# A two-layer graph-attention kernel: x1's transposes and the scalings in another order, queries behind a row's first eaten tile, half of a mask on ScalarE

## The chip, the cores and the metric

The kernel runs on one core of a Trainium2 chip. The metric is the device time of one launch in microseconds. Five engines work side by side, each from a queue of its own that is kept in order, and synchronise by semaphores: TensorE (PE: matrix products and transposes, into PSUM), VectorE (DVE), ScalarE (ACT), GpSimd (POOL) and SyncE (SP), which here issues nearly all DMA transfers. SBUF holds tiles of 128 partitions[...].

## The reference

`x` is (8, 2048, 256) in fp32: eight batch entries of 2048 nodes with 256 features. `adj` is (2048, 2048) of 0 and 1, the same for all entries. Two layers, each with a residual and a layer norm:

```
# layer 0: 8 heads of 32
xp   = einsum('bnd,hdf->bhnf', x, W)
e    = leaky_relu(e_src[..., :, None] + e_dst[..., None, :], 0.2)   # e_src, e_dst = xp . a_src, a_dst
e    = e + softplus(beta) * log(adj + 1e-6);  e = where(adj > 0, e, -big)
h    = softmax(e) @ xp, heads side by side
x    = layernorm(x + h @ W_out.T)
# layer 1: one head of 256
e    = leaky_relu((x @ W1) @ (x @ W2).T, 0.2);  e = where(adj > 0, e, -1e12)
x    = layernorm(x + relu(softmax(e) @ (x @ W3)))
```

## The kernel before, in words

**Layer 0 ("Gat").** The exponential of the leaky sum of two terms is written as a product of factors per row and per column with one maximum, so that the attention of a head is made transposed, source nodes on partitions: a tile `s` for 128 source nodes and half of the target nodes (1024), two heads side by side. A `Unit` is one pair of heads and one half of the targets: 16 such tiles, 8 units per entry. For a tile, ACT scales the transposed mask `mt` by a factor of each head (`scale`, L478, two instructions), DVE takes the maximum with `c` and multiplies (`make`, L492, two), POOL adds the tile to a running sum for the denominator (L498, two), and PE multiplies it with the values (`eat`, L524 `val`). Five of the sixteen tiles (3, 6, 9, 12, 15) are "direct": DVE takes `mt` unscaled, POOL has nothing to do, and PE makes their part of the denominator (`den`). At the end of a unit `close` adds the sum's part (`den` of `ones`), and the values are copied out (L534, L545). The first `make` of a unit needs two copies of `c` into PSUM (L488).

**Layer 1 ("Dot").** A `step` is one row tile of 128 nodes, 16 per entry. `queries` makes h1 for four row tiles (L680, copies L682). `scores` makes a row's scores in four strips of 512 (L691, `e`), each put through leaky relu by ACT (`Prelu`, L693); DVE subtracts the mask and takes the row's maximum (L700), ACT takes the exponential with its sum (L702). `turned` transposes the result (L718, copies L720), and L742 multiplies it with h3 (`acc`). L743 to L750 apply relu, add x1 and take the statistics; `end_row` (L762 to L765) normalises.

**The mask.** Entry 1 of the program (index 0) makes `pen` from `adj` for each row (`mask`, L235 to L243) and stores it; the other entries load it.

**The order.** PE's order is as written in the program throughout. For the first layer of entry 1 a scheduler orders the other engines; from L849 on all engines keep the order of the program. From there a `Stream` feeds the tiles of the next entry's first layer between the instructions of an entry's second layer: `ahead` scales the tile after the next one and makes the next, `eat` multiplies one, `feed` does one of each. `between(c)` stands ahead of a strip's scores, `after(c)` behind its prelu. At the end of an entry stands a seam (L866 to L900): `rows` (L409 `y`, the residual L413, statistics L414) and `rows_scale` and `rows_end` (L420 to L431) make x1 by groups of four row tiles, `turn` transposes x1 (L448, copies L449) and makes h3 from it (L454, copies L456), and `Dot` starts the next second layer with its queries and its first scores, which have no row beside them. `turn` yields after each pair of row tiles; `lag` says by how many pairs h3 follows the transposes.

**Buffers.** `pt`, `e`, `acc`, h1, `y`, `tr` and h3 all take turns in two PSUM banks (tag `mm`, L89), so each of them waits until the tile before the last has been read out; only in the last entry's second layer, when the stream is over, are there six. `s` tiles share a ring of nine with `p` and one half of `ht`; `mt` has four buffers.

Of the kernel before, what the change touches and what calls it, by code (L numbers as in the profile page):

```python
# [9 lines left out]
F32 = mybir.dt.float32  # L10
BF16 = mybir.dt.bfloat16
I32 = mybir.dt.int32
AF = mybir.ActivationFunctionType
# [5 lines left out]
P = 128  # L19
# [1 line left out]
PRIOR_EPS = 1e-6  # L21
LN_EPS = 1e-5
FMAX = 3.4028234663852886e38
NO_EDGE = -3.0e38


@with_exitstack
def kernel(
# [69 lines left out]
    def ring_tile(name, shape=(P, N)):  # L98


        return wide.tile(list(shape), F32, tag="s", name=name, bufs=9)
# [14 lines left out]
    nc.vector.memset(ones, 1.0)  # L116
    eps_ln = const.tile([P, 1], F32)
    nc.vector.memset(eps_ln, LN_EPS)


    beta = const.tile([P, 4], F32)
# [107 lines left out]
    def mask(it, make):  # L229

        pen = wide_tile("pen", "pen", 1, BF16)
        if not make:
            nc.sync.dma_start(pen, pen_d[ts(it, P), :])
            return pen, lambda: None
        edges = [chunk.tile([P, HALF], I32, tag="ht", name="adj_r", bufs=4) for _ in range(2)]  # L235
        for s, a in enumerate(edges):
            nc.sync.dma_start(a, adj[ts(it, P), ts(s, HALF)])

        def put():
            for s, a in enumerate(edges):  # L240
                nc.vector.tensor_scalar(pen[:, ts(s, HALF)], a, 0.0, NO_EDGE, ALU.is_le, ALU.mult)
            nc.sync.dma_start(pen_d[ts(it, P), :], pen)
        return pen, put  # L243

# [16 lines left out]
    class Gat:  # L261


        def __init__(self, b):
            self.b = b
            self.ms, self.mts, self.v = [], [], {}

        def begin(self):

# [89 lines left out]
        def step(self, k):  # L359

            hp, k = divmod(k, NT)
            rh, j2 = divmod(k, J2)
            first = hp == 0
            if hp == NP - 1 and k == 0:
                gats[1].load_factors()
            if j2 == 0:
                self.unit = Unit(self, hp, rh)
            elif j2 == 2:
                stage_after(self.unit)
            if first:  # L370
                self.more_mt(k + 2, k > 0)
            mts = self.mts[k] if first else [load_mt(k, i) for i in range(2)]
            for i in range(2):
                self.unit.scale(2 * j2 + i, mts[i])
# [26 lines left out]
        def rows(self, g):  # L401


            self.load_rows(g + 2)
            self.st = st = small.tile([P, IG // 2, nc.vector.BN_STATS_DIM], F32, name="st4", bufs=2)
            ys = [mm_tile("y").rearrange("p (t c) -> p t c", t=2) for _ in range(IG // 2)]
            for k in range(IG):
                for kc in range(KC):
                    nc.tensor.matmul(ys[k // 2][:, k % 2, :], self.ht[kc][:, ts(g * IG + k, P)], wot[:, kc, :],  # L409
                                     start=(kc == 0), stop=(kc == KC - 1))  # L410
            for k, y in enumerate(ys):
                z = self.x1(2 * g + k)
                nc.vector.tensor_add(z, y, self.xs[g][:, ts(k, 2), :])  # L413
                nc.vector.bn_stats(st[:, k, :], z.rearrange("p t c -> p c t"))  # L414

        def rows_scale(self):

            mv = self.st.rearrange("p a (t c) -> p (a t) c", t=2)
            self.f = f = small.tile([P, 2, IG], F32, name="f4", bufs=2)
            nc.scalar.activation(f[:, 0, :], mv[:, :, 2], AF.Ln, bias=eps_ln, scale=1.0 / D)  # L420
            nc.scalar.activation(f[:, 0, :], f[:, 0, :], AF.Exp, scale=-0.5)
            nc.vector.scalar_tensor_tensor(f[:, 1, :], mv[:, :, 1], -1.0, f[:, 0, :], ALU.mult, ALU.mult)

        def rows_end(self, g):

            for k in range(IG):
                z, f = self.x1(2 * g + k // 2), self.f
                row = z[:, k % 2, :]
                nc.scalar.activation(row, row, AF.Identity, bias=f[:, 1, k:k + 1], scale=f[:, 0, k:k + 1])
                if k % 2:  # L430
                    nc.scalar.dma_start(x1_d[self.b].rearrange("(t p) d -> p t d", p=P)[:, ts(2 * g + k // 2, 2), :], z)  # L431
# [5 lines left out]
        def turn(self):  # L437
# [1 line left out]

            self.x1t = x1t = whole.tile([P, KC, N], F32, tag="x1t", name="x1t")  # L440
            self.h3 = h3 = whole.tile([P, NT, D], F32, tag="h3", name="h3")
            lag = 1 if self.b + 1 < B else 4
            for j in range(NT // 2 + lag):
                if j < NT // 2:
                    t = mm_tile("tr1")
# [15 lines left out]
    class Unit:  # L461
# [7 lines left out]
            self.s, self.mt = {}, {}  # L469
            self.val = self.den = self.sums = None  # L470

        def scale(self, jt, mt):

            self.mt[jt] = mt
            self.s[jt] = s = ring_tile("s", (P, HP, HALF))
            if jt not in self.direct:
                for a, h in enumerate(self.heads):
                    nc.scalar.activation(s[:, a], mt, AF.Copy, scale=self.gat.re[:, 1, jt, h:h + 1])  # L478

        def make(self, jt):  # L480

# [107 lines left out]
    class Stream:  # L589


        def __init__(self):
            self.units = [Unit(gats[b], hp, rh) for b in range(1, B) for hp in range(NP) for rh in range(2)]
            self.count = len(self.units) * NT
            self.loaded = self.scaled = self.made = self.eaten = 0
            self.held = False
            self.mts = {}

        def at(self, n):
# [66 lines left out]
    class Dot:  # L666
# [17 lines left out]
        def scores(self, it, between=lambda c: None, after=lambda c: None):  # L684
# [17 lines left out]
            nc.scalar.activation(p, p, AF.Exp, bias=neg, scale=-1.0, accum_out=den)  # L702
            self.ahead = den

        def step(self, stream, count, lead=0):
# [148 lines left out]
    for b in range(1, B + 1):  # L854
# [19 lines left out]
        for g in range(NB + 2):  # L874
# [61 lines left out]
```

## Time and profile before

| | |
|---|---|
| time, median of three runs | 4374.54 us (4362.75 to 4380.53) |
| the profiled execution's own time | 4372.4 us |
| its span, first to last instruction | 4370.6 us |
| granted TensorE clock, mean | 0.979 of full speed |
| first layer of entry 1 | 0 to about 513 us |
| then an entry's period (seam and 16 rows) | about 505 us |
| an ordinary row | 25.6 us |
| rows of the last entry, without a stream | from 4121 us, 15.5 us each |
| DMA | 843.63 MB, 193 GB/s in the mean |

The profile is of one execution. In the lists a line gives the source line, the engine, the operation and the tiles (out<-in), then how often, the busy time, the mean duration in ns and the idle time of the engine ahead of it with what ended it. In a timeline the columns are start, length, engine and instruction. A matmul in fp32 shows as two records. PE's busy time is modelled to the end of the pipeline, so that a gap of a few tenths between two groups doesn't show.

### The profile page before, as it was taken

Reading aid. Unit: us, or ns where it says so; the run is one execution under the profiler, and the core shown is the slowest. Engines: PE = TensorE matmul, PEld = TensorE weight load, DVE = VectorE, ACT = ScalarE, POOL = GpSimd, SP = SyncE. Lnnn points to the kernel's source line nnn. Section 1 sums busy time; section 2 is a strip of 40 time slices with the busy share of each in tenths; the row PEclk is TensorE's granted clock in tenths of the full one; section 3 lists DMA queues with packets and bytes.
Section 4 is the critical chain, followed back from the end, with each engine's and each line's share of the span. In section 5 each row is a group of like instructions: output and inputs, shape, how many; then the busy total and the mean of one; then the engine's idle time right before and its main releaser. Section 6 shows DMA issues by size and latency. Waiting matters only on the chain.

```text
span 4370.6 us, 60300 instructions
## 1 busy us (share of the span) xinstructions
PE 4126.0 (94%) x22704; PEld 2090.3 (48%) x22704; DVE 3334.9 (76%) x3278; ACT 2905.3 (66%) x4132; POOL 2888.3 (66%) x1190
## 2 busy tenths in 40 slices
PE   7899799998999999999899999999899999999999
PEld 4444344444444444445444454444444444444766
DVE  7888788988878887788777887788787787787222
ACT  6422466676677767677777776677677776776555
POOL 0000477877788887889788877888687887888000
PEclk9999999999999999999999999999999999999999
DMA  8888755666565565556556564656555565554211
GB/s 268 275 288 285 237 198 196 218 223 218 184 198 189 188 205 191 178 195 215 186 178 203 195 207 166 193 193 197 190 199 180 186 219 171 187 192 158 79 46 46
DMA packets 346437, 843.63 MB, mean 193 GB/s; under 512 B 49696, under 2 KB 166432, under 8 KB 346144
## 3 DMA queue, kind: packets, MB, share of 16 engines
q1 hardware_dynamic: 328736, 822.99, 57.4%
q10 hardware_dynamic: 17408, 16.78, 1.1%
q8 instruction: 178, 2.92, 0.3%
q14 instruction: 115, 0.94, 0.1%
HBM read 763.76 MB, written 75.37 MB: 192 GB/s over the span
## 4 chain that ended last, share of the span: by engine, by line
PE 66%; ACT 12%; DVE 9%; issue 6%; DMA 5%; POOL 1%; SPq 1%; ACTq 0%; DVEq 0%; POOLq 0%
PE e L691 18%; PE val L524 15%; PE acc L742 14%; PE den L524 6%; PE pt L718 5%; ACT s L478 5%; DVE s L492 5%; DMA mt<-mt_d 3%; PE h3p L454 3%; DVE p L700 2%; PE h1p L680 2%; ACT p L702 2%; PE y L409 2%; ACT c L488 1%; PE proj L294 1%
## 5 line engine op out<-in xcount | busy, mean ns | idle before, releaser
L498 POOL TENSOR_TENSOR sums<-sums,s 128x1024 f32<-128x1024 f32 x1008 | 2505.7, 2523 | 272.8 <-DVE s L492 271.9
L492 DVE SCALAR_TENSOR_TENSOR s<-c,re,s 128x1024 f32<-128x1024 f32 x1232 | 1500.8, 1272 | 269.9 <-ACT c L488 197.6
L478 ACT ACTIVATE s<-mt,re 128x1024 f32<-128x1024 f32 x1232 | 1339.8, 1140 | 49.9 <-DMA mt<-mt_d 38.7
L524 PE MATMUL val<-s,v 128*32 128x512 f32 x8192 | 1094.5, 607 | 30.7 <-DVE s L492 17.8
L691 PE MATMUL e<-x1t,h 128*128 128x512 f32 x2048 | 995.8, 610 | 45.9 <-ACT pts L720 30.4
L742 PE MATMUL acc<-h,pts 128*128 128x256 f32 x4096 | 918.3, 382 | 1.5 <-ACT pts L720 1.0
L742 PEld LDWEIGHTS acc<-h,pts 128*128 128x128 f32 x4096 | 770.4, 190 | 198.5 <-ACT p L693 29.3
L700 DVE CUSTOM_DVE_ANT_0 p<-p,pen 128x2048 f32<-128x2048 f32 x128 | 459.6, 3591 | 310.3 <-ACT p L693 310.1
L492 DVE SCALAR_TENSOR_TENSOR s<-c,re,mt 128x1024 f32<-128x1024 f32 x560 | 687.5, 1268 | 0.0
L498 POOL TENSOR_TENSOR sums<-s 128x1024 f32<-128x1024 f32 x112 | 291.9, 2629 | 412.4 <-DVE s L492 405.1
L693 ACT ACTIVATE p<-e 128x512 f32<-128x512 f32 x512 | 306.8, 599 | 383.4 <-PE e L691 383.4
L524 PEld LDWEIGHTS val<-s,v 128*32 128x32 f32 x8192 | 203.1, 109 | 683.2 <-issue 442.9
L691 PEld LDWEIGHTS e<-x1t,h 128*128 128x128 f32 x2048 | 356.0, 194 | 333.9 <-issue 258.9
L702 ACT ACTIVATE p<-p,neg 128x2048 f32<-128x2048 f32 x128 | 256.5, 2004 | 374.2 <-DVE neg L700 373.6
L524 PE MATMUL den<-s,re 128*32 128x512 f32 x3264 | 443.1, 594 | 0.0
L718 PEld LDWEIGHTS pt<-ident,p 128*128 128x128 f32 x2048 | 224.1, 142 | 456.0 <-ACT p L693 129.1
L718 PE MATMUL pt<-ident,p 128*128 128x128 f32 x2048 | 332.7, 287 | 73.1 <-ACT p L702 39.5
L492 DVE SCALAR_TENSOR_TENSOR s<-c_in,re,mt 128x1024 f32<-128x1024 f32 x256 | 310.2, 1277 | 51.6 <-DMA mt<-mt_d 39.5
L720 ACT COPY pts<-pt 128x512 f32<-128x512 f32 x512 | 294.5, 579 | 79.8 <-PE pt L718 79.0
L305 POOL PARTITION_ALL_REDUCE top<-top x8 | 6.6, 821 | 428.9 <-DVE top L304 412.5
L524 PEld LDWEIGHTS den<-s,re 128*32 128x32 f32 x3264 | 110.1, 110 | 244.6 <-issue 242.9
L745 DVE TENSOR_TENSOR z<-acc,x1r 128x256 f32<-128x256 f32 x128 | 54.0, 422 | 199.0 <-ACT acc L743 189.8
(96 smaller groups left out, 2493.7 us busy)
## 6 DMA issues: line engine op xcount, KB each, us to landing
mt<-mt_d SPq DMA_DIRECT2D x992, 512.0 KB
c_in<-c_d SPq DMA_DIRECT2D x64, 1024.0 KB
pen<-pen_d SPq DMA_DIRECT2D x112, 512.0 KB
xg<-in_x_dram SPq DMA_DIRECT2D x60, 512.0 KB
adj_t<-in_adj_dram SPq DMA_DIRECT2D x16, 1024.0 KB
mt_d<-mt SPq DMA_DIRECT2D x32, 512.0 KB
rb<-rec_d SPq DMA_DIRECT2D x128, 128.0 KB
x_d<-ht ACTq DMA_DIRECT2D x64, 256.0 KB
```

Source lines behind the costliest of these rows:

```text
L454: nc.tensor.matmul(t[:, ts(i, D)], x1t[:, kc, ts(2 * (j - lag) + i, P)], w3s[:, kc, :], start=(kc == 0), stop=(kc == KC - 1))
L478: nc.scalar.activation(s[:, a], mt, AF.Copy, scale=self.gat.re[:, 1, jt, h:h + 1])
L492: nc.vector.scalar_tensor_tensor(s[:, a], self.c[a], self.gat.re[:, 0, jt, h:h + 1], m, ALU.max, ALU.mult)
L498: nc.gpsimd.tensor_tensor(self.sums[:, a], of[:, a], s[:, a], ALU.add)
L524: nc.tensor.matmul(dst[ts(q, DH), :], weights[q % 2], s[:, q % 2, ts(q // 2, BK)], start=start, stop=stop)
L691: nc.tensor.matmul(t, self.h1[:, kc, ts(it % IG, P)], self.x1t[:, kc, ts(c, BK)], start=(kc == 0), stop=(kc == KC - 1))
L693: nc.scalar.activation(p[:, ts(c, BK)], t, AF.Prelu, alpha=ALPHA)
L700: nc.vector.tensor_tensor_reduce(p, p, pen, -1.0, FMAX, ALU.add, ALU.min, neg)
L702: nc.scalar.activation(p, p, AF.Exp, bias=neg, scale=-1.0, accum_out=den)
L718: nc.tensor.transpose(t[:, ts(k, P)], p[:, ts(g * IG + k, P)], ident)
L720: nc.scalar.copy(pt, t)
L742: nc.tensor.matmul(acc, pts[g][:, ts(k, P)], self.h3[:, j, :], start=(j == 0), stop=(j == NT - 1))
```

## The change

It has these parts, all of them from L849 on.

- **Scaling by head.** `Unit.scale` is split: `begin` takes the slot, `scale(jt, a)` scales one head. `Stream.scale_head` scales the first head of the next tile, `scale_next` what is left of it. In `step`, for strips 1 to 3 of the next row's scores, `scale_head` stands between the transposes' copy and that strip's prelu; the second head comes after the prelu as before. After the last strip, between the row's maximum and the exponential, one more whole tile is scaled (`scale_next(2)`), so that the next `ahead` finds nothing to scale.
- **Queries.** h1 for the next four row tiles is made in the step before it is needed, after the row's first eaten tile, not at the start of the step.
- **Mask.** The mask is positive now (3e38 where there is no edge) and subtracted. For entry 1 ACT makes the first half by a relu of `3e38 - 3e38 * adj`, DVE the second. DVE takes the maximum of the difference and negates it in an instruction of its own, one per row; the exponential loses its scale of -1.
- **Seam.** In `rows` the two residual additions come ahead of both statistics. The factor (L422), so far issued in `rows_scale`, is issued in the next group's `rows` between them, or in `rows_end`. For g > 1 a pair of transposes stands ahead of `ahead(1)`, not behind it, and h3 lags by two pairs where it lagged by one.

```diff
-NO_EDGE = -3.0e38
+NO_EDGE = 3.0e38
...
         def put():
-            for s, a in enumerate(edges):
-                nc.vector.tensor_scalar(pen[:, ts(s, HALF)], a, 0.0, NO_EDGE, ALU.is_le, ALU.mult)
+            nc.scalar.activation(pen[:, ts(0, HALF)], edges[0], AF.Relu, bias=no_edge, scale=-NO_EDGE)
+            nc.vector.tensor_scalar(pen[:, ts(1, HALF)], edges[1], 0.0, NO_EDGE, ALU.is_le, ALU.mult)
...
                 nc.vector.tensor_add(z, y, self.xs[g][:, ts(k, 2), :])
-                nc.vector.bn_stats(st[:, k, :], z.rearrange("p t c -> p c t"))
+            self.rows_factor()
+            for k in range(len(ys)):
+                nc.vector.bn_stats(st[:, k, :], self.x1(2 * g + k).rearrange("p t c -> p c t"))
...
-            nc.vector.scalar_tensor_tensor(f[:, 1, :], mv[:, :, 1], -1.0, f[:, 0, :], ALU.mult, ALU.mult)
+
+        def rows_factor(self):
+
+            if self.mv is not None:
+                nc.vector.scalar_tensor_tensor(self.f[:, 1, :], self.mv[:, :, 1], -1.0, self.f[:, 0, :], ALU.mult, ALU.mult)
+                self.mv = None
 
         def rows_end(self, g):
 
+            self.rows_factor()
...
-            lag = 1 if self.b + 1 < B else 4
+            lag = 2 if self.b + 1 < B else 4
...
-        def scale(self, jt, mt):
+        def begin(self, jt, mt):
 
             self.mt[jt] = mt
-            self.s[jt] = s = ring_tile("s", (P, HP, HALF))
+            self.s[jt] = ring_tile("s", (P, HP, HALF))
+
+        def scale(self, jt, a):
+
             if jt not in self.direct:
-                for a, h in enumerate(self.heads):
-                    nc.scalar.activation(s[:, a], mt, AF.Copy, scale=self.gat.re[:, 1, jt, h:h + 1])
+                h = self.heads[a]
+                nc.scalar.activation(self.s[jt][:, a], self.mt[jt], AF.Copy, scale=self.gat.re[:, 1, jt, h:h + 1])
...
-        def scale_next(self):
-
-            if self.scaled < min(self.made + 1 + AHEAD, self.count):
+        def scale_head(self, ahead=AHEAD):
+
+            if self.heads == 0 and self.scaled < min(self.made + 1 + ahead, self.count, self.eaten + SLOTS):
                 assert self.scaled - self.eaten < SLOTS
                 unit, jt = self.at(self.scaled)
-                unit.scale(jt, self.mts.pop(self.scaled))
+                unit.begin(jt, self.mts.pop(self.scaled))
+                unit.scale(jt, 0)
+                self.heads = 1
+
+        def scale_next(self, ahead=AHEAD):
+
+            self.scale_head(ahead)
+            if self.heads:
+                unit, jt = self.at(self.scaled)
+                for a in range(1, HP):
+                    unit.scale(jt, a)
+                self.heads = 0
                 self.scaled += 1
...
-            nc.vector.tensor_tensor_reduce(p, p, pen, -1.0, FMAX, ALU.add, ALU.min, neg)
+            nc.vector.tensor_tensor_reduce(p, p, pen, 1.0, -FMAX, ALU.subtract, ALU.max, neg)
+            nc.vector.tensor_scalar(neg, neg, -1.0, None, ALU.mult)
             after(NB - 1)
-            nc.scalar.activation(p, p, AF.Exp, bias=neg, scale=-1.0, accum_out=den)
+            nc.scalar.activation(p, p, AF.Exp, bias=neg, accum_out=den)
...
-                if (it + 1) % IG == 0:
-                    self.queries((it + 1) // IG)
-                self.scores(it + 1, turned, lambda c: stream.feed())
+                self.scores(it + 1, lambda c: (turned(c), stream.scale_head() if c else None), lambda c: (stream.feed(), stream.scale_next(2) if c == NB - 1 else None))
...
             stream.eat(1)
+            if (it + 2) % IG == 0 and it + 2 < NT:
+                self.queries((it + 2) // IG)
             stream.ahead(behind - (2 if it + 1 == NT else 1) + lead)
...
             stream.eat(1)
-            stream.ahead(1)
             if g > 1:
                 next(turns)
+            stream.ahead(1)
```

More of the change, by code (lines that the diff above doesn't have):

```diff
@@ L118 @@
     nc.vector.memset(eps_ln, LN_EPS)
+    no_edge = const.tile([P, 1], F32)
+    nc.vector.memset(no_edge, NO_EDGE)
     beta = const.tile([P, 4], F32)
@@ L265, in __init__ @@
             self.b = b
-            self.ms, self.mts, self.v = [], [], {}
+            self.ms, self.mts, self.v, self.mv = [], [], {}, None
         def begin(self):
@@ L373, in step @@
             for i in range(2):
-                self.unit.scale(2 * j2 + i, mts[i])
+                self.unit.begin(2 * j2 + i, mts[i])
                 self.unit.make(2 * j2 + i)
@@ L413, in rows @@
                 nc.vector.tensor_add(z, y, self.xs[g][:, ts(k, 2), :])
-                nc.vector.bn_stats(st[:, k, :], z.rearrange("p t c -> p c t"))
+            self.rows_factor()
+            for k in range(len(ys)):
+                nc.vector.bn_stats(st[:, k, :], self.x1(2 * g + k).rearrange("p t c -> p c t"))
         def rows_scale(self):
-            mv = self.st.rearrange("p a (t c) -> p (a t) c", t=2)
+            self.mv = mv = self.st.rearrange("p a (t c) -> p (a t) c", t=2)
             self.f = f = small.tile([P, 2, IG], F32, name="f4", bufs=2)
@@ L595, in __init__ @@
             self.loaded = self.scaled = self.made = self.eaten = 0
-            self.held = False
+            self.held, self.heads = False, 0
             self.mts = {}
```

## The prediction

> **What bounds the kernel now.** I read the page's busy shares first, then the table of stretches, then TensorE's own waits, then the timeline of one seam and one row. The page's first part:
>
> ```profile
> PE 4126.0 (94%) x22704; PEld 2090.3 (48%) x22704; DVE 3334.9 (76%) x3278; ACT 2905.3 (66%) x4132; POOL 2888.3 (66%) x1190
> ```
>
> TensorE (PE) is the bound, and no matmul is removed, so the change can only win PE's idle time: 4370.6 - 4126.0 = 244.6 us. The table of stretches (length; busy of PE, PEld, DVE, ACT, POOL; clock) says where that lies:
>
> ```profile
> 623.00:1045.00 422.00, 392.49 (x2087) 188.38 (x2086) 373.79 (x348) 289.17 (x395) 340.18 (x135) 0.98 0.66 217
> 1159.00:1549.00 390.00, 381.99 (x2089) 186.12 (x2089) 317.65 (x317) 290.56 (x396) 333.04 (x135) 1.00 0.61 196
> 2553.00:2667.00 114.00, 99.55 (x536) 50.65 (x536) 87.23 (x80) 74.31 (x110) 77.27 (x35) 0.93 0.55 183
> 4053.00:4121.00 68.00, 67.32 (x298) 50.67 (x297) 18.39 (x35) 37.56 (x76) 2.35 (x1) 1.00 0.31 97
> ```
>
> Fifteen rows of a plain entry leave PE 8 us idle, those of entry 1 (which also make the mask) 29.5 us with DVE 89% busy, a seam between entries 14.5 us, the last seam nothing. By the same table all plain rows together idle 55 us, the seven seams 101. PE's own waits (total, times, longest):
>
> ```profile
> PE h3p L454 <- ACT x1t L449: 40.4, 7, 7.6
> PE pt L718 <- ACT p L702: 39.5, 8, 6.4
> PE e L691 <- ACT pts L720: 30.4, 7, 6.8
> PE pt L718 <- ACT h L682: 13.8, 7, 4.1
> PE e L691 <- DVE z L745: 12.1, 12, 1.5
> PE y L409 <- DVE ht L413: 7.6, 6, 2.7
> PE val L524 <- ACT ht L545: 7.3, 5, 2.8
> ```
>
> The first two are the seams, once each. The timeline of one:
>
> ```profile
> 2583.82 0.63 PE L448 MATMUL tr<-ident,ht 128*128 128x128 f32 x4 [0.70 <-DVE ht L413]
> 2584.90 0.59 ACT L534 COPY first<-val 128x512 f32<-128x512 f32 x1 [0.44 <-ACT ht L429]
> 2585.38 1.97 ACT L488 COPY c<-c_in 128x1024 f32<-128x1024 f32 x2
> 2587.27 2.19 ACT L478 ACTIVATE s<-mt,re 128x1024 f32<-128x1024 f32 x2
> 2589.36 1.06 ACT L449 COPY x1t<-tr 128x512 f32<-128x512 f32 x2
> 2589.98 3.78 PE L454 MATMUL h3p<-w3s,x1t 128*128 128x256 f32 x8 [5.53 <-ACT x1t L449]
> ```
>
> The x1t copies stand behind 4.2 us of other ScalarE (ACT) work; the eight matmuls after the gap take 3.78 us, twice their usual 1.89. And a row:
>
> ```profile
> 2977.33 2.17 ACT L478 ACTIVATE s<-mt,re 128x1024 f32<-128x1024 f32 x2
> 2979.53 0.45 ACT L743 ACTIVATE acc<-acc,rec 128x256 f32<-128x256 f32 x1
> 2980.01 0.42 DVE L745 TENSOR_TENSOR z<-acc,x1r 128x256 f32<-128x256 f32 x1 [1.27 <-ACT acc L743]
> 2980.49 1.98 PE L691 MATMUL e<-x1t,h 128*128 128x512 f32 x4 [0.90 <-DVE z L745]
> ```
>
> Two PSUM banks serve all these tiles, so e waits for z to free acc's bank, z for L743, and L743 for a scaled tile.
>
> **What the Trainium skill says.** "SBUF — State Buffer", Who interferes with whom: a VectorE (DVE) operation with two SBUF inputs shuts out, or is shut out by, a GpSimd (POOL) operation that reads SBUF; one input outside the two-port modes does not. The trace agrees: L700 takes 2.29 us in the tail, where POOL is idle, and up to 7.8 beside it; L422 0.16 to 3.86; the one-column L750 always 0.15. "ScalarE: Activation LUTs", What ACT_TABLE_LOAD costs, gives 186 ns + 0.833 ns per element and 93 ns per pointer operand: for the new mask 1.13 us, an estimate, near L478's 1.14. "TensorE: Matmul & The Clock Gate", What's actually happening, says the array runs at half rate after about 3.4 us idle until 3.4 us busy; the 3.78 us above agree.
>
> **The change, part by part.** Groups concerned (busy, mean ns, idle before):
>
> ```profile
> L241 DVE TENSOR_SCALAR pen<-adj_r 128x1024 bf16<-128x1024 int32 x32 | 70.3, 2232 | 8.5 <-DMA adj_r<-in_adj_dram 8.4
> L745 DVE TENSOR_TENSOR z<-acc,x1r 128x256 f32<-128x256 f32 x128 | 54.0, 422 | 199.0 <-ACT acc L743 189.8 <-DMA x1r<-x_d 9.2
> ```
>
> *Heads around prelu, and the extra tile before exp.* ACT issues the same scales. In a strip it does copy 0.46, prelu 0.49, two heads 2.08 = 3.03 us (starts at 1525.45 to 1528.48) against PE's 3.33, so ACT is on time for the next prelu either way; a head ahead of prelu fills the 1.1 us in which ACT waits for e. Between the last prelu and exp ACT now does three heads, 3.2 us, inside L700's 3.59 us mean. With the tile that stood between exp and L743 gone, L743 comes up to 2.2 us earlier, and z, which waits 189.8 us for it, with it. This answers the waits on z (12.1) and on L545 (7.3), where a scale stood ahead as well. The mt tile is wanted one tile (25.6 / 7 = 3.7 us) sooner; its load is issued two makes earlier, so I cost that at nothing; were it late, exp would slip, which has about 5 us before its transposes (exp ends at 1511.85, pt starts at 1517.30).
>
> *Queues.* SP's and POOL's instructions keep their order; only what they wait for moves. The row's store on SP waits for L765 behind exp, and the mt loads behind it with it, by the negation's 0.2 us. Scaling a tile sooner asks for its slot of the ring sooner: POOL's adds follow the tile's L492 by 3.5 to 13.6 us, the slot comes round after seven tiles, 25.6 us, so I cost that at nothing too.
>
> *Queries after the first eaten tile.* The same 8 matmuls, 3.4 us, and two copies, with three tiles (2.7 us or more) between them and the pt that needs their banks: answers 13.8. The second h1 tile must now wait for z, which is early. The three answers sum to 33.2; I take three quarters, since DVE's own order stays: -25. The 30.4 stays: there z stands behind four L492 after the c copies, in either order.
>
> *Mask.* Entry 1 loses one L241 of two per row, 16 x 2.2 = 35 us of DVE, and gains 16 x 1.14 = 18 us of ACT, 69% busy there. Its rows are 422 - 392.6 = 29.4 us longer than the mean of the plain ones; less the 5 of h1 counted above I take half: -12. (Bounds: 0 to -24.) On ACT the mask stands ahead of a head, a copy and the last prelu; that prelu, 1.1 us late, holds no bank that PE wants before the next row, and L700, which waits for it, now has one L241 less ahead of it on DVE.
>
> *Negation.* 128 x (0.15 + about 0.05) us between L700 and exp, hidden by exp's 5 us; in the tail PE is dense. Uncovered it would be +26. I take 0.
>
> *Adds before bn_stats, factor later.* Both y banks are freed without the locked L422 (up to 3.86 us) or a bn_stats (0.71) ahead: y's 7.6 and, of the transposes' small waits on L413 and L429 (3.5 and 4.4), some: -10. The price: a factor now waits for the next y group, so L429 and what ACT queues behind it (x1t, h, scales, and through these DVE's tiles) wait too. For groups 0 and 1 ACT waits no longer than now: there the lock or L421 ends last. For group 2 I lay it out: y ends, add 0.7, factor, about 5 us in which ACT stands idle, and again 2 us before group 3's L429, less 2.7 us that ACT gained by not waiting for h3p: +2.5 per seam (0 to +6).
>
> *Transposes first, lag 2.* The 5.5 us wait for x1t goes, but the next thing is late: the first tile of the new unit needs the c copies, which now stand behind the x1t copies (+1.05). PE then waits from its earlier tr to about 2590 for val instead of h3p. Laid out to y(3), PE is 2.9 us ahead with one h3p (1.8) fewer done: -1.1. That h3p moves into the hole after the first scores (6.4), -1.8, but its copy stands between exp and pt, +0.6, with the negation's +0.2: -1.0. Seam: 2.5 - 1.1 - 1.0 = +0.4, times seven = +3. The last seam has no tiles to fill in: tr of groups 1 and 2 waits for the later factor, +2.5.
>
> Sum: -25 - 12 + 0 - 10 + 3 + 2.5 = -41.5. The profiled execution took 4372.4 us (span 4370.6 and 1.8 around it): 4330.9. The median, 4374.54, is 2.1 above it: 4333.
>
> **Rivals.** A half per cent, 22 us, is about what a measurement of this kernel can tell from no change.
> *The seam pays* (0.25). The first L700 of a seam takes 7.7 us behind three GpSimd adds in five seams of seven, but 3.1 and 3.5 in the others. If its new place meets a gap, 5 x 4.6 = 23, and with shorter gaps the half-rate stretches (about 1.6 x 7 = 11) go: 4297. Against: the same adds still precede it.
> *The factor costs its upper bound* (0.15): +35 in place of most of +3 gives about 4365; rows gain, seams give it back. For: L429 waits 35.8 us for L422 already.
> *Head ahead of prelu is late* (0.13; slower). e of the next strip needs prelu's bank 1.4 us after e ends, and prelu takes 0.6: 0.8 us of slack. 112 rows x 3 strips x 11/16 = 231 heads stand ahead of a prelu. Where ACT comes late (c copies 2 us, L545 1.2) or mt has not landed, each adds up to 1.04. It eats the gain at 0.18 us per head and is slower by half a per cent from 0.27; at 0.35 (+81) 4414. Against: in strips ACT waits for e, not the reverse (383 us).
> *The change does nothing that PE sees* (0.04): 4374.
>
> **How the numbers follow.** My forecast has 0.43, its own range 4310 to 4352. Faster than 4352.6: 0.43 + 0.25 = 0.68; between, 0.15 + 0.04 = 0.19; slower, 0.13. From the seam case with 22 us of its own spread, 4275, to 4392, which leaves out the late heads: 8 in 10.
>
> **What would show it.** Right: waits of e on z and of pt on h L682 near nothing; entry 1's rows near 405 us; h3p's wait on x1t gone, a wait of val on DVE or of tr on ACT in its place, seam length within 3 us; L429's wait on L422 above 35.8. Wrong: ACT's 383 us for e smaller while PE's waits on prelu grow (late heads), or seams 5 us shorter with an L700 near 3.5 us.

## The result, and the profile after

| | median us | runs | profiled execution | PE busy | PE idle |
|---|---|---|---|---|---|
| before | 4375.95 | 4 (4362.75 to 4380.53) | 4372.4, span 4370.6 | 4126.0 | 244.6 |
| after | 4309.6 | 4 (4305.87 to 4324.04) | 4305.9, span 4304.1 | 4111.9 | 192.2 |

The changed kernel is faster: ratio 0.9859, 95% interval 0.9828 to 0.9891. The time lies inside the stated range (4275 to 4392), 23 us below the forecast and just under the forecast's own range (4310 to 4352).

The page's first part, after:

```profile
PE 4111.9 (96%) x22704; PEld 2073.5 (48%) x22704; DVE 3257.0 (76%) x3391; ACT 2932.1 (68%) x4148; POOL 2910.7 (68%) x1190
```

The same 22704 matmuls took 14.1 us less, and PE's idle time fell by 52.4. The table of stretches (length; busy of PE, PEld, DVE, ACT, POOL; clock), for entry 1's rows, a plain entry's rows, a seam and the last seam:

```profile
628.00:1022.00 394.00, 381.94 (x2092) 184.77 (x2088) 338.31 (x346) 305.84 (x410) 340.26 (x136) 1.00 0.71 231
1133.00:1518.00 385.00, 380.67 (x2092) 184.83 (x2088) 312.44 (x331) 291.84 (x395) 335.13 (x135) 1.00 0.62 198
2515.00:2627.00 112.00, 100.86 (x537) 50.10 (x536) 81.02 (x82) 75.57 (x112) 79.40 (x35) 0.97 0.58 188
3993.00:4055.00 62.00, 59.00 (x255) 43.31 (x254) 14.72 (x32) 32.56 (x68) 2.35 (x1) 1.00 0.32 104
```

Entry 1's rows leave PE 12 us idle in place of 29.5, and their PE busy time fell from 392.5 to 381.9 for the same work, as the clock rose from 0.98 to 1.00. A plain entry leaves 4.3 in place of 8, a seam 11.1 in place of 14.5.

Measured from the start of one row's acc to the next (the first acc of an entry to its last: fifteen steps), both profiled executions divide like this:

| stretch | before | after | difference |
|---|---|---|---|
| start to the first acc, first seam included | 622.7 | 628.4 | +5.7 |
| entry 1, fifteen steps | 422.8 | 393.9 | -28.9 |
| entries 2 to 6 (plain), mean | 392.5 | 385.7 | 5 x -6.8 |
| entry 7, the last with tiles beside its rows | 377.3 | 372.5 | -4.8 |
| six seams (last acc of an entry to first acc of the next), mean | 112.8 | 111.6 | 6 x -1.2 |
| last seam | 59.0 | 61.4 | +2.4 |
| entry 8 (no tiles beside its rows) | 236.4 | 236.4 | 0 |

The sum, -66, is the whole difference of the two profiled executions: it lies in the rows, hardly in the seams. PE's own waits, after:

```profile
PE val L537 <- DVE s L505: 74.9, 26, 10.5
...
PE e L715 <- ACT p L717: 11.4, 13, 0.9
PE pt L743 <- ACT h L466: 8.8, 7, 1.6
PE e L715 <- ACT pts L745: 8.5, 7, 3.2
...
PE e L715 <- DVE z L768: 0.5, 2, 0.3
```

Gone are h3p on x1t (40.4), pt on exp (39.5) and pt on the queries' copies (13.8). e on pts fell from 30.4 to 8.5. In place of the first two, which were the seams' waits, stands val on VectorE's tiles, 74.9 us (17.8 before). Of it 52 us lie in the seven seams, 6.2 to 6.7 us at the turn to the new unit in six of them and 10.5 in the first; the rest lies in the first layer of entry 1. The timeline of one seam:

```profile
2548.22 1.99 ACT L501 COPY c<-c_in 128x1024 f32<-128x1024 f32 x2
2549.30 7.24 DVE L505 SCALAR_TENSOR_TENSOR s<-c,re,s 128x1024 f32<-128x1024 f32 x6 [4.46 <-ACT c L501]
2550.11 2.20 ACT L491 ACTIVATE s<-mt,re 128x1024 f32<-128x1024 f32 x2
2550.64 2.26 PE L537 MATMUL val<-s,v 128*32 128x512 f32 x5 [6.25 <-DVE s L505]
```

This is the seam as the forecast drew it: PE waits from its tr to about 2550.6 for the new unit's first tile, whose c copies stand behind the x1t copies.

### The profile page after: what moved, and what is told of

The parts are those of the page before. It is cut to its first block, busy times and chain, and to the rows that moved or that the text cites. A ratio compares the mean times of both kernels' runs of the same rounds, so it can differ in the third digit from the quotient of the medians.

```text
span 4304.1 us, 60568 instructions
## 1 busy us (share of the span) xinstructions
PE 4111.9 (96%) x22704; PEld 2073.5 (48%) x22704; DVE 3257.0 (76%) x3391; ACT 2932.1 (68%) x4148; POOL 2910.7 (68%) x1190
## 4 chain that ended last, share of the span: by engine, by line
PE 71%; ACT 10%; DVE 7%; DMA 6%; issue 4%; SPq 1%; ACTq 1%; POOL 0%; DVEq 0%; POOLq 0%
PE acc L765 18%; PE e L715 18%; PE val L537 16%; PE den L537 6%; PE pt L743 5%; ACT s L491 4%; DVE s L505 4%; DMA mt<-mt_d 3%; PE h1p L704 3%; PE y L411 2%; DVE p L724 2%; PE proj L296 1%; ACT c L501 1%; ACT ht L439 1%; PE h3p L464 1%
## 5 line engine op out<-in xcount | busy, mean ns | idle before, releaser
L491 ACT ACTIVATE s<-mt,re 128x1024 f32<-128x1024 f32 x1232 | 1358.7, 1143 | 92.8 <-DMA mt<-mt_d 76.2
L537 PE MATMUL val<-s,v 128*32 128x512 f32 x8192 | 1116.0, 607 | 81.6 <-DVE s L505 74.9
L715 PE MATMUL e<-x1t,h 128*128 128x512 f32 x2048 | 973.2, 598 | 20.7 <-ACT p L717 11.4
L724 DVE CUSTOM_DVE_ANT_0 p<-p,pen 128x2048 f32<-128x2048 f32 x128 | 415.8, 3248 | 357.0 <-ACT p L717 356.9
L743 PEld LDWEIGHTS pt<-ident,p 128*128 128x128 f32 x2048 | 220.2, 141 | 424.1 <-ACT p L717 148.4
L743 PE MATMUL pt<-ident,p 128*128 128x128 f32 x2048 | 328.6, 284 | 36.8 <-ACT pts L745 28.0
L298 ACT COPY v<-proj 128x512 f32<-128x512 f32 x64 | 37.2, 585 | 186.1 <-PE proj L296 135.9
```

The costliest lines, as they stand in the source:

```text
L491: nc.scalar.activation(self.s[jt][:, a], self.mt[jt], AF.Copy, scale=self.gat.re[:, 1, jt, h:h + 1])
L537: nc.tensor.matmul(dst[ts(q, DH), :], weights[q % 2], s[:, q % 2, ts(q // 2, BK)], start=start, stop=stop)
L715: nc.tensor.matmul(t, self.h1[:, kc, ts(it % IG, P)], self.x1t[:, kc, ts(c, BK)], start=(kc == 0), stop=(kc == KC - 1))
L724: nc.vector.tensor_tensor_reduce(p, p, pen, 1.0, -FMAX, ALU.subtract, ALU.max, neg)
L743: nc.tensor.transpose(t[:, ts(k, P)], p[:, ts(g * IG + k, P)], ident)
```

## The experiments

Two readings serve every kernel below: the median, and the two stretches defined above (seam = mean of six; rows = fifteen steps). The start up to the first acc lies between 617 and 630 us in the fourteen profiles, though hardly anything in it differs but the first seam; so differences of up to some 8 us between two medians are not put down to a cause unless the rows or seams show it. The kernel before took 4377.4, 4369.8 and 4376.8 in the three groups of runs.

### Each part taken out of the changed kernel

**The seam.** Lag 1, a tile ahead of the transposes, bn_stats beside each add, the factor at once:

```diff
             for k, y in enumerate(ys):
                 z = self.x1(2 * g + k)
                 nc.vector.tensor_add(z, y, self.xs[g][:, ts(k, 2), :])
-            self.rows_factor()
-            for k in range(len(ys)):
-                nc.vector.bn_stats(st[:, k, :], self.x1(2 * g + k).rearrange("p t c -> p c t"))
+                nc.vector.bn_stats(st[:, k, :], z.rearrange("p t c -> p c t"))
...
             nc.scalar.activation(f[:, 0, :], f[:, 0, :], AF.Exp, scale=-0.5)
+            self.rows_factor()
...
-            lag = 2 if self.b + 1 < B else 4
+            lag = 1 if self.b + 1 < B else 4
...
+            stream.ahead(1)
             if g > 1:
                 next(turns)
-            stream.ahead(1)
```

> The changed kernel with its seam as before: lag 1, a tile ahead of the transposes, bn_stats beside each add, the factor at once. All else stays. Forecast's ledger (adds -10, seam +3, last seam +2.5): 4.5 us come back, about 4314; seams from 111.7 to about 112, the wait of h3p on x1t back at 40 us and that of val on DVE (74.9) down by about 43. Rival, that the seam pays more than forecast (its rows end earlier and leave shorter gaps at half rate): 113.3 mean of the seven seams as in the kernel before against 111.7, so +11 to +17, less 2.4 of the last seam: 4319 to 4325. If the seven seams come out at 111.7 or less, the seam part gave nothing.

Measured: 4317.0 (4309.0 to 4327.2), 7.4 us slower; seams 113.5 in place of 111.6, last seam 59.1; h3p on x1t 40.6 and pt on exp 44.3 back, val on DVE 19.0. The part as a whole is worth little, as the forecast said (4.5). What it is made of comes below.

**The queries.**

```diff
+                if (it + 1) % IG == 0:
+                    self.queries((it + 1) // IG)
                 self.scores(it + 1, ...)
...
-            if (it + 2) % IG == 0 and it + 2 < NT:
-                self.queries((it + 2) // IG)
```

> The changed kernel with the queries back ahead of the first strip of the row. Forecast's ledger (three quarters of the wait of pt on h, 13.8): 10 us come back, about 4320, in the rows it = 3, 7 and 11 of each entry (29.4, 30.9 and 30.3 us now). Rival 1, that the scales moved earlier already free ACT for the copies of the queries: within 3 us of the changed kernel. Rival 2, that queries in a row are worth more with the scales moved, since the bank of pt is asked for sooner: 20 us or more.

Measured: 4298.4 (4293.9 to 4309.9), 11.2 us *faster* than with the move. Between the two profiled executions it is 10.1, of which 6 lie in the start, which the move doesn't touch. In the plain entries the rows at which queries stand are 29.6, 29.7 to 30.3 and 30.5 in place of 29.4, 30.9 and 30.3. PE's waits for the queries' copies, in this kernel:

```profile
PE pt L743 <- ACT h L706: 4.7, 3, 3.3
```

With the queries at their old place this wait is 4.7, not 13.8: another part of the change had answered most of it. Rival 1 holds: the move is worth nothing, or a little less than nothing (the second of these rows, where a unit turns over, is some 1 us longer with it).

**The mask.** Both halves on VectorE again:

```diff
-            nc.scalar.activation(pen[:, ts(0, HALF)], edges[0], AF.Relu, bias=no_edge, scale=-NO_EDGE)
-            nc.vector.tensor_scalar(pen[:, ts(1, HALF)], edges[1], 0.0, NO_EDGE, ALU.is_le, ALU.mult)
+            for s, a in enumerate(edges):
+                nc.vector.tensor_scalar(pen[:, ts(s, HALF)], a, 0.0, NO_EDGE, ALU.is_le, ALU.mult)
```

> The changed kernel with both halves of entry 1's mask on VectorE, positive fill and negation kept. Forecast's ledger: 12 us come back, entry 1's fifteen rows from 394 to 406, total about 4322. Rival, that the whole of entry 1's gain of 28 us over the plain rows' 5 to 9 is the mask's: rows back to about 415, total about 4330, with the granted clock of this stage back from 1.00 to 0.98. Lower bound: nothing, if the tile moved ahead of exp had given VectorE the room: 4310.

Measured: 4314.4 (4312.7 to 4324.5), 4.8 slower; entry 1's rows 398.2 in place of 393.9. Neither 406 nor 415.

**The scales.** Whole tiles behind each prelu, no extra tile ahead of exp:

```diff
-                self.scores(it + 1, lambda c: (turned(c), stream.scale_head() if c else None), lambda c: (stream.feed(), stream.scale_next(2) if c == NB - 1 else None))
+                self.scores(it + 1, turned, lambda c: stream.feed())
```

> The changed kernel with whole tiles scaled behind each prelu as before, and no extra tile ahead of exp (so both halves of that part undone). Forecast's ledger (three quarters of e on z 12.1 and val on ht 7.3, and the unit-turn stall of e on pts stays as it is): 15 us come back, about 4325, wait of e on pts still 8.5. Rival, that this part also removed the unit-turn stall, because the tile that stood between exp and the relu of acc was one of the four things ahead of pts: e on pts back at about 30 us, rows at a unit's turn 30 to 33 us instead of 27 and 30.9, total 4340 to 4350.

Measured: 4358.5 (4346.7 to 4364.4), 48.9 slower. Rows are 406.9 in entry 1, 393.5 in plain ones, and two of PE's waits are back:

```profile
PE e L715 <- ACT pts L745: 25.7, 7, 5.6
PE e L715 <- DVE z L768: 15.2, 13, 1.7
```

This part is most of the gain, and the rival is right: it also removed the stall at a unit's turn. PE's busy time went from 4111.9 to 4135.9 with it, so of the 54 us between the two profiled executions 24 are the same matmuls taking longer.

### Which half of the scales

The head ahead of prelu taken out, the extra tile kept (first kernel), and the tile taken out, the head kept (second):

```diff
-                self.scores(it + 1, lambda c: (turned(c), stream.scale_head() if c else None), lambda c: (stream.feed(), stream.scale_next(2) if c == NB - 1 else None))
+                self.scores(it + 1, turned, lambda c: (stream.feed(), stream.scale_next(2) if c == NB - 1 else None))
```

```diff
-                self.scores(it + 1, lambda c: (turned(c), stream.scale_head() if c else None), lambda c: (stream.feed(), stream.scale_next(2) if c == NB - 1 else None))
+                self.scores(it + 1, lambda c: (turned(c), stream.scale_head() if c else None), lambda c: stream.feed())
```

> The changed kernel with no head ahead of prelu (whole tiles behind it), but with the extra tile scaled ahead of exp. The two together gave 49 us. If the tile out of the way of the relu of acc is what pays: within 10 us of 4309.6, wait of e on z near nothing, e on pts near 8.5. If the head ahead of prelu is what pays (STT of the next tile can start one head earlier, so VectorE's last prelu-to-TTR stretch begins on time): 4340 to 4358, the rows of entry 1 back at 407.

> The changed kernel with the head ahead of prelu but no extra tile ahead of exp, so that a tile stands between exp and the relu of acc again. If that tile is what costs: 4340 to 4358, e on z 12 to 15 us and e on pts 25 us back. If the head ahead of prelu is what pays: within 10 us of 4309.6.

Measured: without the head 4303.3 (4300.9 to 4309.0); without the tile 4372.2 (4363.9 to 4386.3), no different from the kernel before (ratio 0.9999, 0.9988 to 1.0011). PE's waits without the tile:

```profile
PE e L715 <- ACT pts L745: 25.4, 7, 5.8
PE e L715 <- ACT p L717: 18.0, 24, 1.1
PE e L715 <- DVE z L768: 12.2, 11, 1.7
```

The tile alone carries the gain: 63 us with the head in place (4372.2 to 4309.6), 55 without (4358.5 to 4303.3). The head gives nothing beside the tile, and without it costs 14 (4358.5 to 4372.2): PE then waits 18 us for prelu, longest 1.1, the length of one head. How the tile pays is seen in the fifth row of an entry, where a unit turns over; the seven waits of e on pts are these rows, one in each entry with tiles beside it. ScalarE, VectorE and PE, before:

```profile
2782.85 1.94 ACT L488 COPY c<-c_in 128x1024 f32<-128x1024 f32 x2
2784.73 2.18 ACT L478 ACTIVATE s<-mt,re 128x1024 f32<-128x1024 f32 x2
2786.82 0.42 ACT L743 ACTIVATE acc<-acc,rec 128x256 f32<-128x256 f32 x1
...
2788.46 0.59 ACT L720 COPY pts<-pt 128x512 f32<-128x512 f32 x1
2788.67 0.41 DVE L745 TENSOR_TENSOR z<-acc,x1r 128x256 f32<-128x256 f32 x1
2789.10 3.78 PE L691 MATMUL e<-x1t,h 128*128 128x512 f32 x4 [5.78 <-ACT pts L720]
```

and the same row after:

```profile
2739.10 1.94 ACT L501 COPY c<-c_in 128x1024 f32<-128x1024 f32 x2
...
2740.98 0.44 ACT L766 ACTIVATE acc<-acc,rec 128x256 f32<-128x256 f32 x1
...
2742.63 0.58 ACT L745 COPY pts<-pt 128x512 f32<-128x512 f32 x1
2743.27 1.98 PE L715 MATMUL e<-x1t,h 128*128 128x512 f32 x4 [1.02 <-ACT pts L745]
...
2744.91 0.41 DVE L768 TENSOR_TENSOR z<-acc,x1r 128x256 f32<-128x256 f32 x1
```

The copy of pts comes 5.6 us after the start of the c copies in the first, 3.5 us after it in the second. The tile's 2.2 us are gone from this chain; they are spent earlier, under the long mask-and-maximum operation of VectorE. Before, PE stood idle 5.8 us ahead of e here and then took 3.78 us for four matmuls; after, 1.0 and 1.98. And e began 1.6 us before z: in this row e does not wait for z at all. So the two banks do not simply take turns here, as "Buffers" has it: e waits for the tile just before it, pt, and in both kernels it is ScalarE's semaphore on which it waits in this row.

### What the seam is made of

The factor at once, at the end of rows_scale, all else as changed (first kernel):

```diff
             nc.scalar.activation(f[:, 0, :], f[:, 0, :], AF.Exp, scale=-0.5)
+            self.rows_factor()
```

and besides the old transposes (lag 1, and the tile ahead of them, as in the first diff above), so that only the adds ahead of bn_stats remain (second kernel):

> The changed kernel with only the deferral of the seam's factor undone: it is computed straight after the two small operations of ScalarE that it needs, as before; adds still ahead of bn_stats. Forecast's ledger (+2.5 per seam and +2.5 in the last): 20 us faster than the changed kernel, about 4290, seams near 109.3, the last near 59. Rival 1, that the factor at once meets GpSimd's adds and holds the adds of the next y for up to 3.9 us in group 0 of each seam: seams within 1 us of 111.7, y on ht back at 8 to 10 us, total within 5 of 4309, the last seam alone 2.4 shorter. Rival 2: slower by 5 or more, if the seams go to 112.5 and over.

> The changed kernel with the factor at once and the old place and lag of the transposes, so that of the seam's part only the two adds ahead of the two bn_stats are left. The whole seam part gave 7.4 us (4317.0 without it), and without the deferral it gives 36 (4280.9). Forecast's split (adds -10, transposes and lag -2.1 a seam and so -15 in the seven): 4317 - 10 = 4307, seams about 112.3. Rival, that the transposes' place and lag are nothing, as one wait takes the place of another: about 4281. Rival on the other side, that the adds give nothing: 4317.

Measured: factor at once 4280.9 (4277.7 to 4284.4), 28.7 faster than the changed kernel; adds only 4307.9 (4306.2 to 4310.7). From 4317.0 (nothing of the seam part) the steps are adds -9.2, transposes and lag -27.0, deferral +28.7. Of the adds' 9.2 the seams show 5 (113.5 to 112.7, six times), and the ranges of the two kernels touch. The transposes were taken out beside the factor at once alone, not beside the deferral. ScalarE's wait for the factor, in the changed kernel and with the factor at once:

```profile
ACT ht L439 <- DVE f L430: 94.1, 31, 5.9
```

```profile
ACT ht L440 <- DVE f L431: 32.4, 14, 6.3
```

The factor itself is 1.39 us in the median of 32 with the factor at once (longest 4.49) and 0.16 (longest 2.14) in the changed kernel: deferred, it mostly escapes GpSimd, but ScalarE waits for it longer all the same.

Why the transposes gave more than two waits changing places can give is in the first mask-and-maximum of a seam. VectorE and GpSimd with the adds only, and then with the change whole:

```profile
2595.48 6.96 POOL L512 TENSOR_TENSOR sums<-sums,s 128x1024 f32<-128x1024 f32 x3
2596.75 7.84 DVE L725 CUSTOM_DVE_ANT_0 p<-p,pen 128x2048 f32<-128x2048 f32 x1 [2.31 <-ACT p L718]
```

```profile
2601.93 6.76 POOL L511 TENSOR_TENSOR sums<-sums,s 128x1024 f32<-128x1024 f32 x2
2602.67 3.77 DVE L724 CUSTOM_DVE_ANT_0 p<-p,pen 128x2048 f32<-128x2048 f32 x1 [2.31 <-ACT p L717]
```

In the first, three adds of 2.3 us run to their end before VectorE gets its turn; in the second it gets it after one, and the next add takes 4.5. In six seams it took 7.84 to 7.88 with the adds only, and 3.77 to 3.79 with the change. With the factor at once it took 2.7 in four seams and 7.37 in two. One of each kind:

```profile
1589.39 7.00 POOL L512 TENSOR_TENSOR sums<-sums,s 128x1024 f32<-128x1024 f32 x3
1591.17 7.37 DVE L725 CUSTOM_DVE_ANT_0 p<-p,pen 128x2048 f32<-128x2048 f32 x1 [2.31 <-ACT p L718]
```

```profile
2585.90 9.13 POOL L512 TENSOR_TENSOR sums<-sums,s 128x1024 f32<-128x1024 f32 x3
2587.71 2.72 DVE L725 CUSTOM_DVE_ANT_0 p<-p,pen 128x2048 f32<-128x2048 f32 x1 [2.31 <-ACT p L718]
```

In the combination below it took 2.69 in one and 7.35 to 7.37 in five. Sorting the twelve seams of these two kernels by it: seven with the long one are 112.9 us in the mean (111.1 to 114.3), five with the short one 107.8 (105.6 to 108.9). The difference, 5.1, is about that of the operation (4.6). Which of the two a seam gets is called its draw below. Five other kernels have such a draw too: in the kernels with the mask on VectorE, without the scales, without the head, without the tile and with the unit early one seam of six had 6.1 us there in place of 3.8, two adds in place of one, and was 1.4 to 3.1 us longer than the mean of the others. So with the long one the transposes' new place gives nothing (112.9 against 112.7 with the adds only), and with the short one all of its gain.

### The mask part alone, on the kernel before

Positive fill, one half on ScalarE, subtract and max, the negation:

```diff
...
-            nc.vector.tensor_tensor_reduce(p, p, pen, -1.0, FMAX, ALU.add, ALU.min, neg)
+            nc.vector.tensor_tensor_reduce(p, p, pen, 1.0, -FMAX, ALU.subtract, ALU.max, neg)
+            nc.vector.tensor_scalar(neg, neg, -1.0, None, ALU.mult)
...
```

> The kernel before with the mask part alone: positive fill, half of entry 1's mask on ScalarE, the subtract and max form and the negation. Forecast's ledger: -12 for the mask and 0 for the negation, so about 4358 to 4363, entry 1's rows from 422.7 to about 410. Rival, from taking the part out of the changed kernel (4.8 us): about 4366 to 4370, rows about 418; then entry 1's other 20 us came from the tile moved ahead of exp. If the negation costs what it would uncovered (+26), the plain rows get longer by 3 each entry and the total passes 4375.

Measured: 4373.3 (4360.5 to 4383.6), ratio 0.9990 (0.9978 to 1.0002): not to be told from nothing. Yet entry 1's rows are 408.2 in place of 422.8, about as forecast. The plain rows are 394.2 (392.5 before) and the seams 114.1 (112.8). Three rows of each plain entry are 0.3 us longer throughout, which is the size of the negation (0.15) and its passing; in the seams the long operation is part of it (the one seam of 108.8 before had a short one, 3.08; here all six took 7.7). The negation was not run by itself, so its share stays open; it is below 2 us per entry.

### Two better versions

The next unit begun earlier in the changed kernel, then the three parts that did not pay taken out, then both, with only the c copies moved:

```diff
+            if g == 1 and dot:
+                stream.ahead(2)
             if 0 < g <= NB:
                 gat.rows_end(g - 1)
...
             if g > 1:
                 next(turns)
-            stream.ahead(1)
+            if not (dot and 0 < g < 3):
+                stream.ahead(1)
```

The combination has the factor at once, the queries at their old place and no head ahead of prelu, by the diffs above. With the c copies early, the code of make for tile 0 that copies c becomes a method of its own, take, and is called sooner:

```diff
+            if g == 1 and dot and stream.made < stream.count:
...
+                stream.at(stream.made)[0].take()
             if 0 < g <= NB:
                 gat.rows_end(g - 1)
```

> The changed kernel with the next unit begun earlier in each of the seven seams: its two c copies and first two tiles are issued behind the second group's adds and ahead of that group's end of rows, where ScalarE waits 5.4 us for the factor, in place of one group later, behind the x1t copies. Theory that the c copies' place is now what the seam waits for (val on s 74.9 us, 10.5 and 6.2 us a seam): that wait falls by 40 us or more, seams 105 to 108, total 4265 to 4285. Rival, that the rows' factor is late in any order and the transposes are next: val's wait turns into waits of tr on ht L439 and of h3p on x1t, seams within 2 us of 111.7. Slower (4320 and over) if the two tiles on VectorE hold the adds of the third y group.

> The changed kernel with what its parts did not pay taken out: factor at once (28.7 us faster alone), queries at their old place (11.2 faster alone), no head ahead of prelu (6.3 faster alone). If these add up: 4309.6 - 46 = 4263. If queries and heads are within what draws of GpSimd's lock scatter (about 8 us): 4275 to 4283, as the factor alone.

> The kernel before this one in the list, with the two c copies of the next unit issued ahead of the first group's end of rows in each seam of entries (six of them), while the first tiles stay in their place. Beginning the unit early gave 10.5 us to the changed kernel. If val's wait for the first tile behind those copies (4 to 7 us a seam) is what is left: 15 to 30 us faster than without, 4235 to 4265. If the copies, which wait for the old unit's last tile, hold the end of rows by their 2 us: within 5 us of the kernel without.

Measured: unit early 4299.2 (4288.1 to 4306.8), seams 109.7, val on DVE 28.4 with 19.3 of val on the copy of first in its place: 10 faster, less than expected. The combination 4281.9 (4276.9 to 4298.1), as fast as the factor alone; what was taken out besides is within the scatter. Its profiled execution, the slowest of its four, drew the long operation in five of six seams. With the c copies early 4251.8 (4246.2 to 4273.0): 30 us faster again, ratio to the kernel before 0.9728 (0.9695 to 0.9761), seams 106.0. Part of the shorter seams is the draw, since the long operation stands in two of six here. Like for like these two are 108.3 in place of the 112.9 above, and the other four 104.8 in place of 107.8: 3 to 4.6 us per seam, some 21 of the 30, are the copies. Its seam:

```profile
2504.44 5.11 DVE L431 SCALAR_TENSOR_TENSOR f<-st,f 128x4 f32<-128x4 f32 x1
2504.58 1.02 ACT L502 COPY c<-c_in 128x1024 f32<-128x1024 f32 x1 [0.17 <-DVE s L511]
...
2509.64 1.09 ACT L440 ACTIVATE ht<-ht,f 128x256 f32<-128x256 f32 x2 [4.05 <-DVE f L431]
...
2519.32 1.69 PE L543 MATMUL val<-s,v 128*32 128x512 f32 x5 [0.84 <-ACT first L553]
```

The copies now lie where ScalarE waits for the factor anyway, which in this seam took VectorE 5.11 us, and PE waits 0.84 us for val in place of the 6.25 of the changed kernel's seam above.

## Why the prediction was right or wrong

**Right in sign and in the stated range, but not by its own sum.** Forecast -41.5 against -66.5 between the profiled executions. The range reached down to 4275 for a rival in which the seams pay; the gain beyond the forecast came from the rows, where no rival looked for it. That the range held is in part luck. So is the seam part's small sum: its transposes gave more than forecast and its deferral cost more. In what follows, where medians are used, a part is put at the changed kernel's 4309.6 less the median of the kernel without it, so that a minus means time saved.

**Heads, tile and queries: "This answers the waits on z (12.1) and on L545 (7.3)", "answers 13.8", together -25.** Half of the mechanism was right: the tile out of the way of L743 frees z (12.1 to 0.5). The step that failed is "The 30.4 stays: there z stands behind four L492 after the c copies, in either order". The reading of z was right: it stayed behind four operations of VectorE, as the row above shows. But in this row e did not wait for z. It waited for the copy of pts, which stands on ScalarE behind the tile and came 2.1 us nearer. 22 of the 30.4 went. The 13.8 were credited to the queries, but with the scales moved only 4.7 are left without that. And the sum counted idle time only. Over the rows of the seven entries PE's idle time fell from 84.7 to 40.3 us and its busy time, for the same matmuls, from 2677.9 to 2654.7. "The change can only win PE's idle time" was wrong by this. The prediction had quoted a slow stretch (3.78 us for 1.89) that follows 5.5 us of idle time, and the Trainium skill ("TensorE: Matmul & The Clock Gate", What's actually happening) says that the array runs at half rate after a long idle spell; the sum left it out. Not every gap gives this back: in the six seams idle time fell from 80.3 to 66.8 while busy time rose from 596.6 to 603.1, for a reason that the runs don't settle. Measured: the whole scales part -48.9, the tile in it -62.6, the head +6 to +14, the queries 0 to +11.

**Mask, -12.** Right for entry 1's rows when the part is taken alone: 14.6 shorter, with the half on ScalarE at the 1.14 us that was estimated (16 of them). In company it is worth 4.3, since the tile moved ahead of exp cures part of the same lateness: with everything but the tile these rows are 408.4, as with the mask alone (408.2), and with both 393.9, not 405. The parts' losses when taken out one by one add up to 49.9 of 66; overlaps of this kind, and the scatter of the medians, are the rest.

**Negation, 0.** Not the 26 of the uncovered case; some 0.3 us in three rows of an entry. Not isolated.

**mt's load, nothing.** ScalarE's wait for mt rose from 38.7 to 76.2 us, and in the row after a unit's turn exp slipped by some 0.7 us for it (VectorE done at 2787.8, exp at 2788.5). No wait of PE for pt on exp is left in the changed kernel.

**Adds, -10.** Measured -9.2 between medians, of which the seams show 5; PE's wait for VectorE ahead of y went from 10.6 to 5.0.

**Deferral, +2.5 per seam, +2.5 in the last.** The two seam lengths are 109.1 and 111.6, the last 58.7 and 61.4: +2.5 and +2.7. The price was right, though a mean over draws: with the short kind of operation in both (2.7 and 3.8), it is 107.8 against 111.6. In medians the whole effect is 28.7. Between the profiled executions it is 21.5: 18 in the seven seams, 7 in the start, where the first seam is one of the causes and scatter another, and -3 in the rows.

**Transposes, -1.1 and -1.0 per seam.** The exchange of waits is as forecast: h3p on x1t gone, val on DVE in its place, the h3p in the hole (pt on h L466, 8.8). By length it came to -3.6 per seam with the factor at once (112.7 to 109.1), and the mechanism was the rival's: the first long VectorE operation got its turn after one add of GpSimd or after three. "Against: the same adds still precede it" did not hold: they do, but at another distance.

**The rivals.** "The seam pays" (4297) named the right operation: 7.7 us in five of the six seams before, 3.8 in all six with the change. But the deferral took most of that back, so seams fell by 1.2. The factor's upper bound: its price in medians, 28.7, lies between the forecast's 20 and this rival's 35, but the rows gained more. The late head was seen in sign: PE's wait on prelu, not among its waits before, is 11.4 us (18.0 without the tile) and ScalarE's wait for e fell from 383 to 260; its price, by the dearer of the two measurements, is 14 us / 231 = 0.06 per head, a third of the 0.18 from which it would have decided.

## What to carry to other kernels

Follow the engine queue that a waiting matmul's operand really stands in: here a 2.2 us tile between exp and the copies was worth 63 us, since it stood ahead of three things that PE wanted in turn (the relu of acc, the copies of a unit's values, the copy of pts), and what was put there instead lay under an operation of VectorE that ran anyway. Parts of one change that cure the same lateness don't add up, and a sum of waits leaves out the matmuls that run slowly after a long one. Take each part out once the whole has paid: without three of the parts, and with two copies moved into a wait that was already there, the kernel is 58 us faster than the change as made.

## What the runs showed of the hardware

- The VectorE operation with two inputs in SBUF (2.29 us alone) is not simply delayed by the GpSimd add under way. Asked for 0.58 us ahead of the end of an add it let that add and two more pass (7.37); in another seam of the same execution, asked for 0.56 us ahead, it got its turn at the end of the first (2.72), and the next add took 4.5 in place of 2.4. The Trainium skill ("SBUF — State Buffer", Who interferes with whom) says that they shut each other out. How often the turn is missed decides some 5 us of a seam. Only one execution of each kernel was profiled, so whether the draw changes from one execution to the next was not seen.
- The factor, of four columns, took from 0.15 to 6.24 us (the longest in the kernel without the seam part), and GpSimd's work decides it. In that kernel and the one with the factor at once, the 22 factors asked for with nothing under way on GpSimd took 0.16 to 0.17 us. Of the 42 asked for during one of its operations 34 ended with it, seven one operation later and one two later.
- Entry 1's rows needed 10.6 us less of PE for the same matmuls once most of their gaps were gone (392.5 to 381.9, with the granted clock at 0.98 and 1.00).
